# Two fixed PSUM tiles for the decays of a selective scan, each half in a bank of its own

## The chip, the core and the metric

The kernel runs on one core of one Trainium2 chip. The metric is the device time of one execution in microseconds; the figure quoted for a kernel is the median of several runs. A profile is one further execution, recorded by the hardware profiler. The engines are named as in the profile: PE (matrix products), PEld (its weight loads), DVE (vector engine), ACT (scalar engine), POOL (GpSimd), SP (the queue that issues DMAs).

## What is computed

Two layers follow each other on 32 images of 128 channels and 56 x 56 pixels, all in fp32. Layer 0 is a 7 x 7 depthwise convolution, a normalisation over channels and a routed mixture of eight small networks. Layer 1, which the change touches, holds a selective scan (Mamba) over the 3136 pixels of an image, with 256 inner channels and a state of 16 per channel:

```python
dA = jnp.exp(dt[..., None] * A)                      # decays, per channel, state and pixel
dBu = dt[..., None] * Bm[:, :, None, :] * xm[..., None]
def step(h, inp):
    dA_t, dBu_t, C_t = inp
    h = dA_t * h + dBu_t
    return (h, jnp.einsum('bds,bs->bd', h, C_t))
...
y = ys.transpose(1, 0, 2) + xm * D
return y * jax.nn.silu(z) @ out_proj_w.T
```

Around it lie a 1 x 1 convolution, a 3 x 3 depthwise branch, normalisations, Silu and softplus, and a last 1 x 1 convolution with the residual.

## The kernel before

Layer 0 runs first and leaves its result in `res_d`. `layer1` then cuts each image into 7 groups of 448 pixels (`CH1`), 224 groups in all. A group has 16 units, one for each state index (`DS`), so there are 3584 units. The 256 channels are two halves of 128 partitions; a unit's data are therefore 128 x 898: two halves of 449 elements (`W1`), the first element of each half being a carry from the group before.

One unit u passes through five steps:

- `db_pool` (line 1006, POOL) multiplies `du` and a broadcast row `bb` into `dbs[i]`, one of 16 fixed SBUF tiles, four units ahead.
- `exp_act` (line 1012, ACT) makes the decays `da`, in PSUM, with two activations, one for each half. `da` comes from the pool `pda`, which has two buffers of two banks. Half 0 fills elements 0 to 448, half 1 elements 449 to 897.
- `scan_dve` (line 1021, DVE) runs the recurrence over all 898 elements. For the ten units that are not in `POOL_C` it writes in place, into `da`. For the six units in `POOL_C` (0, 4, 6, 7, 12, 15) it writes to `hs` in SBUF.
- `cmul` (line 1027) multiplies by the broadcast row `cb` into `prod`: on DVE for in-place units, on POOL for `POOL_C` units.
- `carry_act` (line 1033, ACT) copies the last element of each half into `dbs[i]`, for the next group; in the last group of an image it copies zeros and so reads neither `da` nor `hs`. `sum_pe` (line 966, PE) adds up the products in PSUM (`py`).

The order of the work is written out by hand, step by step of a loop over t, and each engine keeps that order:

```python
if valid(t - 1):
    carry_act(t - 1)
if valid(t + 4):
    db_pool(t + 4)
if valid(t + 1):
    exp_act(t + 1)
if valid(t):
    scan_dve(t)
    if i not in POOL_C:
        cmul(t, nc.vector)
```

So in ACT's order the decays of unit t + 1 follow the carry of unit t - 1, whose buffer they can take over. The other work of a group is put into this order by `at(offset, function)`: among it `silus` (lines 837 to 854: a table load on ACT, two activations into `xm`, the product `p_z` on PE at line 843, three activations, a second table load) at unit 2 of the group before, `sp_act` (line 919, the two halves of `dt`) at unit 11, `lt_act` (line 950) at unit 13, `te_dve` (line 805, DVE) at unit 14, `yz_dve` (line 958, DVE) at unit 4. [...]

[...]

## Time and profile before

| what | value |
|---|---|
| median of 3 runs | 16874.84 us (16873.99 to 16886.92) |
| the profiled execution, its own time | 16882.28 us |
| its span, first to last instruction | 16880.3 us |
| mean granted TensorE clock | 0.905 |
| first scan begins, last scan ends | 6169.6 us, 16868.1 us |
| exponentials, line 1012 | 7168 x 639 ns |
| scans in place / into hs, line 1021 | 2240 x 2021 ns / 1344 x 2014 ns |
| products on DVE / on POOL, line 1027 | 2240 x 1092 ns / 1344 x 1932 ns |
| db on POOL, line 1006 | 3584 x 1936 ns |

In a row of the profile's groups the columns are line, engine, operation, output and inputs, shapes and count, then the busy time in us and the mean of one in ns, and last the idle time of that engine just ahead of these instructions with what ended most of it. In a timeline the columns are the start and the duration in us, engine, line, operation, and in brackets the idle time ahead of it.

### The profile page before, as it was taken

The page shows a single profiled execution, that of the slowest core. Times are in us where ns is not written, and L with a number is a line of the kernel's source. Part 1 is how long each engine was busy: PE and PEld are TensorE (multiplying, and loading weights), DVE is VectorE, ACT ScalarE, POOL GpSimd, SP SyncE. Part 2 cuts the span into 40 slices and gives each one's busy share as a digit, 9 for nine tenths or more (in the row PEclk, how much of TensorE's full clock was granted, in tenths as well). Part 3 has the DMA queues.
Part 4 walks back from the last instruction along what each step waited for, and adds up shares of the span by engine and source line. Part 5 has one row for each costly group of instructions (what it writes and reads, how often), then busy time and mean ns, then how long its engine had stood idle before and what let it go on. Part 6 is the DMA issues. An engine that isn't in the chain of part 4 may idle for free. (4 is left out here: it accounts for less than half of the span.)

```text
span 16880.3 us, 246139 instructions
## 1 busy us (share of the span) xinstructions
PE 12727.3 (75%) x91548; PEld 7010.5 (42%) x91548; DVE 11290.7 (67%) x10141; ACT 10542.4 (62%) x20754; POOL 13634.4 (81%) x9015
## 2 busy tenths in 40 slices
PE   5996200000999988888888888888888888888888
PEld 4996000000777744443444433444443444443443
DVE  1564800000111149999999999999999999999998
ACT  3564000000444458888888888888888888888887
POOL 1343067777888879999999999999999999999998
PEclk8997555555999999999999999999999999999999
DMA  9879032222555545555555555555555555555554
GB/s 255 239 231 228 7 99 84 82 85 64 70 72 71 70 101 169 171 171 168 171 172 169 171 170 170 170 171 170 172 170 170 169 171 170 172 170 170 169 171 157
DMA packets 1360754, 2533.24 MB, mean 150 GB/s; under 512 B 139119, under 2 KB 805339, under 8 KB 1355456
## 3 DMA queue, kind: packets, MB, share of 16 engines
q1 hardware_dynamic: 1163072, 2361.89, 45.3%
q0 software_dynamic: 196480, 155.61, 6.0%
q8 instruction: 720, 11.80, 0.3%
q14 instruction: 482, 3.95, 0.1%
HBM read 2180.38 MB, written 375.43 MB: 151 GB/s over the span
## 5 line engine op out<-in xcount | busy, mean ns | idle before, releaser
L1006 POOL TENSOR_TENSOR db<-du,bb 128x896 f32<-128x896 f32 x3584 | 6852.0, 1936 | 17.6
L1012 ACT ACTIVATE da<-dt,aneg 128x449 f32<-128x449 f32 x7168 | 4576.9, 639 | 603.0 <-DVE hs L1021 340.5
L1021 DVE TENSOR_TENSOR_SCAN da<-da,db 128x898 f32<-128x898 f32 x2240 | 4528.0, 2021 | 275.3 <-ACT da L1012 273.9
L1027 POOL TENSOR_TENSOR prod<-hs,cb 128x896 f32<-128x896 f32 x1344 | 2596.1, 1932 | 698.4 <-PE p_cvc L736 579.0
L966 PE MATMUL py<-prod,ident 64*64 64x448 f32 x28672 | 3099.4, 545 | 23.3 <-POOL prod L1027 16.5
L1021 DVE TENSOR_TENSOR_SCAN hs<-da,db 128x898 f32<-128x898 f32 x1344 | 2671.4, 2014 | 450.4 <-ACT db L1033 407.1
L1027 DVE TENSOR_TENSOR prod<-da,cb 128x896 f32<-128x896 f32 x2240 | 2445.7, 1092 | 216.2 <-issue 2.7
L516 ACT COPY xc<-ept 128x512 f32<-128x512 f32 (+1 forms) x248 | 144.1, 581 | 2922.6 <-DMA xb<-buf_d 2034.0
L425 POOL DMA_INDIRECT buf_d<-xg,slot x1568 | 1536.6, 980 | 485.7 <-issue 476.6
L474 POOL DMA_INDIRECT res_d<-ys,xb x984 | 1587.2, 1613 | 338.6 <-issue 286.7
L514 PE MATMUL ept<-ident,xb 128*128 128x128 f32 (+1 forms) x984 | 188.7, 274 | 2033.3 <-DMA xb<-buf_d 2033.3
L966 PEld LDWEIGHTS py<-prod,ident 64*64 64x64 f32 x28672 | 1046.2, 132 | 1444.3 <-issue 1173.5
L821 PE MATMUL p_xm<-te,wk 128*128 128x448 f32 x3584 | 1410.3, 544 | 12.3 <-DVE te L805 1.9
L422 DVE COPY xg<-gate 128x28 f32<-128x28 f32 x56 | 11.5, 233 | 1792.6 <-DMA buf_d<-xg,slot 1792.6
L466 DVE TENSOR_TENSOR ys<-py,b2t 128x512 f32<-128x512 f32 (+2 forms) x256 | 170.9, 670 | 1477.0 <-PE py L460 1269.3
L460 PEld LDWEIGHTS py<-w2t,hh 128*128 128x128 f32 x7872 | 936.2, 191 | 175.6 <-issue 113.3
L460 PE MATMUL py<-w2t,hh 128*128 128x128 f32 x7872 | 985.0, 278 | 0.3
L514 PEld LDWEIGHTS ept<-ident,xb 128*128 128x128 f32 (+1 forms) x984 | 124.6, 143 | 2037.0 <-issue 2036.9
L180 PE MATMUL pc<-xc,toep 112*112 112x112 f32 (+1 forms) x8192 | 935.8, 270 | 45.5 <-ACT toep L169 41.9
L821 PEld LDWEIGHTS p_xm<-te,wk 128*128 128x128 f32 x3584 | 657.5, 189 | 750.6 <-issue 543.1
L180 PEld LDWEIGHTS pc<-xc,toep 112*112 112x112 f32 x8192 | 881.4, 184 | 54.9 <-ACT toep L169 48.9
L210 POOL TENSOR_TENSOR xa<-xa,lng 112x896 f32<-112x896 f32 x128 | 267.3, 2088 | 773.2 <-ACT xa L207 709.7
(235 smaller groups left out, 19677.3 us busy)
## 6 DMA issues: line engine op xcount, KB each, us to landing
bb<-bc_d SPq DMA_DIRECT2D x1792, 448.0 KB
cb<-bc_d SPq DMA_DIRECT2D x1792, 448.0 KB
toep<-toep_d SPq DMA_DIRECT2D x448, 392.0 KB
xg<-res_d SPq DMA_DIRECT2D x56, 1792.0 KB
buf_d<-zero SPq DMA_DIRECT2D x14, 4550.0 KB
xb<-buf_d SPq DMA_DIRECT2D x240, 260.0 KB
xt<-in_x SPq DMA_DIRECT2D x32, 1568.0 KB
res_d<-xa SPq DMA_DIRECT2D x128, 392.0 KB
```

The source lines that it names most:

```text
L180: nc.tensor.matmul(pc[:, c, :, lo:hi], lhsT=tp[c // 2][:, c % 2, 6 - 2 * o : 8 - 2 * o, :], rhs=s4[:, c, :, lo + o - 1 : hi + o - 1], star ...
L210: nc.gpsimd.tensor_tensor(xa, xa, lng.unsqueeze(1).to_broadcast([TT, w, C]), ALU.mult)
L425: apart(nc.gpsimd.indirect_dma_start(out=buf_d[:, :], out_offset=bass.IndirectOffsetOnAxis(ap=slots[k][:, q, p0 + j : p0 + j + 1], axis=0) ...
L460: nc.tensor.matmul(py[:n, j, :], lhsT=hh[:, k, j * 128 : j * 128 + n], rhs=w2t[:, k, :], start=k == 0, stop=k == KF - 1,)
L474: apart(nc.gpsimd.indirect_dma_start(out=res_d[:, :], out_offset=bass.IndirectOffsetOnAxis(ap=xb[:n, j, C + 1 : C + 2].bitcast(I32), axis= ...
L514: nc.tensor.transpose(pt[:, j * 128 : j * 128 + n], xb[:n, j, :C], ident[:n, :n])
L821: nc.tensor.matmul(p[:, :CH1], lhsT=s["wk"][:, k, hs], rhs=d["te"][:, k : k + CH1], start=k == 0, stop=k == DC - 1 and not first,)
L966: nc.tensor.matmul(ps[r][h * HD : (h + 1) * HD, :CH1], lhsT=lhsT(rs, h), rhs=rhs[rs, h, :], start=start, stop=stop,)
L1006: nc.gpsimd.tensor_tensor(dbv[i][:, :, 1:], st[g]["du"], units[u].pop("bb"), ALU.mult)
L1012: nc.scalar.activation(da[:, h * W1 : (h + 1) * W1], st[g]["dt"][:, h, :], AF.Exp, scale=s["aneg"][:, h, i : i + 1])
L1021: nc.vector.tensor_tensor_scan(hs, da, dbs[i], 0.0, ALU.mult, ALU.add)
L1027: eng.tensor_tensor(w["prod"], w["hs"][:, :, 1:], w.pop("cb"), ALU.mult)
```

## The change

`pda` no longer rotates two buffers of one name. It holds two tiles with names of their own for the whole of layer 1, and unit u uses tile u % 2. Of each tile's 1024 elements[...] the 898 from element 63 to 960 are used[...]. The exponentials, the scan, the product and the carry work on the same shapes as before.

```diff
-        tc.tile_pool(name="pda", bufs=2, space=PSUM) as pda,
+        tc.tile_pool(name="pda", bufs=1, space=PSUM) as pda,
...
+        das = [pda.tile([128, 1024], F32, name=f"da{i}")[:, 512 - W1 : 512 + W1] for i in range(2)]
...
         def exp_act(u):
             g, i = divmod(u, DS)
-            da = units[u]["da"] = pda.tile([128, 1024], F32, name="da")
+            da = das[u % 2]
             for h in range(2):
...
         def scan_dve(u):
             i = u % DS
             w = units[u]
-            da = w.pop("da")[:, : 2 * W1]
+            da = das[u % 2]
```

## The prediction

> **What bounds the kernel now.** The change touches only layer 1's scans, so I first ask where layer 1 lies and which engine sets its pace. The page's first part gives the engines over the whole span:

> ```profile
> PE 12727.3 (75%) x91548; PEld 7010.5 (42%) x91548; DVE 11290.7 (67%) x10141; ACT 10542.4 (62%) x20754; POOL 13634.4 (81%) x9015
> ```

> Layer 1 begins with the first scan at 6169.6 us and its last scan ends at 16868.1, so 10.7 ms of the 16.88 are at stake. There DVE (VectorE) and POOL (GpSimd) both stand at nine tenths in the page's slices. The rows of the costliest groups say which of them waits for which:

> ```profile
> L1006 POOL TENSOR_TENSOR db<-du,bb 128x896 f32<-128x896 f32 x3584 | 6852.0, 1936 | 17.6
> L1012 ACT ACTIVATE da<-dt,aneg 128x449 f32<-128x449 f32 x7168 | 4576.9, 639 | 603.0 <-DVE hs L1021 340.5
> L1021 DVE TENSOR_TENSOR_SCAN da<-da,db 128x898 f32<-128x898 f32 x2240 | 4528.0, 2021 | 275.3 <-ACT da L1012 273.9
> L1027 POOL TENSOR_TENSOR prod<-hs,cb 128x896 f32<-128x896 f32 x1344 | 2596.1, 1932 | 698.4 <-PE p_cvc L736 579.0
> L1021 DVE TENSOR_TENSOR_SCAN hs<-da,db 128x898 f32<-128x898 f32 x1344 | 2671.4, 2014 | 450.4 <-ACT db L1033 407.1
> ```

> The last column is idle time ahead of the group and what ended it. POOL idles 698 us ahead of its products, and no row has DVE waiting for POOL: the decay inputs db lie ready 4 to 12 us before the scan that reads them. So DVE sets the pace and POOL follows. DVE's own idle time has two pieces: 274 us ahead of scans in place, ended by the exponentials (ACT, line 1012), and 450 us ahead of the hs scans, mostly ended by ACT too.

> Now the timeline, first DVE and then ACT, around units 12 and 13 of an ordinary group (columns: start us, us, what, idle before):

> ```profile
> 10028.05 2.02 DVE L1021 TENSOR_TENSOR_SCAN hs<-da,db 128x898 f32<-128x898 f32 x1
> 10031.50 2.04 DVE L1021 TENSOR_TENSOR_SCAN da<-da,db 128x898 f32<-128x898 f32 x1 [1.43 <-ACT da L1012]
> ```
> ```profile
> 10026.47 0.96 ACT L919 COPY dt<-p_sp 128x448 f32<-128x448 f32 x2
> ...
> 10028.17 0.16 ACT L1033 COPY db<-da 128x2 f32<-128x2 f32 x1 [0.46 <-DVE prod L1027]
> 10030.10 1.31 ACT L1012 ACTIVATE da<-dt,aneg 128x449 f32<-128x449 f32 x2 [1.77 <-DVE hs L1021]
> ```

> Unit 11's scan, product and carry are over at 10028.33, so one of the two buffers is free; yet the exponentials of unit 13 sit still for 1.77 us until unit 12's scan ends at 10030.07. That is a claim on unit 12's buffer, not on the free one: the pool has handed out the wrong one of the two, and in the built program it does so for unit 13 in 192 of 224 groups. Unit 13's scan then waits 1.43 us for decays that could have been made beside unit 12's scan. In the last group of each image, whose carries copy zeros, the same place looks different, DVE and ACT again:

> ```profile
> 11171.70 2.02 DVE L1021 TENSOR_TENSOR_SCAN hs<-da,db 128x898 f32<-128x898 f32 x1
> 11173.63 2.01 DVE L1021 TENSOR_TENSOR_SCAN da<-da,db 128x898 f32<-128x898 f32 x1
> ```
> ```profile
> 11171.82 1.31 ACT L1012 ACTIVATE da<-dt,aneg 128x449 f32<-128x449 f32 x2 [0.57 <-DVE prod L1027]
> ```

> Here the exponentials start as soon as unit 11's product ends, and the scans follow each other in 1.93 us. This is a control inside the trace: scan 12 to scan 13 takes 3.451 us in the 192 other groups and 1.934 in these 32. Whole groups (first scan to next first scan) take 47.60 and 45.76.

> The second stall comes when ACT works through the Silu block with its two table loads; the hs scan of unit 4 waits for carry 2 and its own exponentials:

> ```profile
> 10006.64 2.03 DVE L1021 TENSOR_TENSOR_SCAN hs<-da,db 128x898 f32<-128x898 f32 x1 [1.65 <-ACT db L1033]
> ```

> Scan 3 to scan 4 takes 5.86 us there, but up to 7.44 in 83 groups. The two PE timelines show why: the four p_z passes that ACT waits for take 3.07 instead of 1.77 us where the granted clock has dipped (0.58 on average over 11239 to 11243, against 1.00 over 11288 to 11292).

> ```profile
> 11239.33 3.07 PE L843 MATMUL p_z<-te,wz 128*128 128x448 f32 x4 [2.44 <-ACT xm L837]
> ```
> ```profile
> 11288.23 1.77 PE L843 MATMUL p_z<-te,wz 128*128 128x448 f32 x4 [2.44 <-ACT xm L837]
> ```

> [...]the carry (line 1033) only reads da, as the product does, and still waits for it (10028.17 above). [...]two exponentials that share no element are ordered one behind the other: the pair takes 1.31 us with 639 ns each, a gap of 33 ns, where the two dt copies of 529 ns above take 0.96, an overlap of 100. [...]the trace's slow stretches here are 3.41 us long and lie on one grid.

> **The change part by part.**

> Removed: the pool's choice. Unit 13 gets unit 11's buffer always. Its exponentials start behind carry 11 at 10028.36, end by 10029.67, and scan 12 ends at 10030.07: 0.3 us to spare before scan 13's earliest start (10029.98, since it follows an hs scan as in the control). 192 x (3.451 - 1.934) = 291 us; scan 13 itself is 2.036 now against 2.009 in the control, 192 x 0.027 = 5. **-296 us.**

> Who is late next? In the control nothing was: 13 to 14 takes 3.11, 14 to 15 takes 3.65 in both. te, lt and the carries ride on the same chain and move with it. POOL's work fills 44.7 of 47.6 us of a group (2.9 us idle at two products), so it keeps up with 45.9; its lead over the scans shrinks to what the groups behind the control already have, 4.15 us at the least.

> Removed: the wait of half 1 on half 0. An instruction that follows an exponential without a wait starts 0.06 us before its end (10026.47 against 10025.22 + 1.31), so each pair shortens by 33 + 63 = 96 ns. ACT has slack except before unit 4, where the pairs of units 3 and 4 lie on the chain: 2 x 0.096 x 224 = **-43 us**. Bounds: 0 if the wait stays, 43 if it goes.

> Moved: the data start at element 63. ACT's half 1 started at 449 before[...], at the same 639 ns as half 0, so ACT: nothing. [...]yz (line 958), the same shape[...], is 1080 ns against the product's 1092, so 0 to 12 x 2240 = 27 us of gain; I take 0.

> Added, by the new pace: clock dips. 47.60 us are 13.95 windows of 3.413, so undelayed groups drift slowly and mostly stay where PE's 2.44 us pause costs nothing; 83 groups were delayed, 88 us in all, 0.39 a group. Sorted by where scan 3 falls in its window, the delay is nothing over the first 0.42, climbs to 1.58 us at 0.84 and is gone at 0.97: a mean of 0.57 over all positions. A group of 47.60 - 1.54 - 0.19 = 45.87 us is 13.44 windows, so successive groups fall all over the window. Stepping from group to group with that curve gives 0.33 to 0.42 for the old pace (measured 0.39) and 0.58 to 0.68 for the new. I take 0.62: 224 x (0.62 - 0.39) = **+50 us**. Bounds 0.40 to 0.80: +0 to +90.

> **Sum:** -296 - 43 + 50 = -289 us against the profiled execution, 16882.28 us, which is 7.4 above the median of 16874.84. So the median becomes **16586 us**.

> **The rivals.**

> *The stall only moves* (0.03): scan 13 starts earlier but te or exponential 15 is then late by as much. Only the 43 us at unit 4 can remain, less some dips: about 16850, no change that can be measured (0.2%, 34 us, is about the least). Against it: the control.

> *The odd start costs DVE* (0.03, slower): 3584 scans and 2240 products now begin 252 bytes into a bank, and DVE is the bound. From 289 / 5824 = 50 ns each it eats the gain; at 100 ns the time is 16586 + 582 = 17168. For it: no trace row has a scan that starts there. Against: carries, products (from element 1) and ACT's half 1 already have odd starts, with no price to be seen.

> *The clock always dips* (0.05): the new pace settles at 1.58 a group: 224 x (1.58 - 0.39) = +266 in place of +50, 16802, still faster.

> *The halves' wait stays* (0.1): 16629, inside the range.

> **How the numbers follow.** The forecast with its bounds has 0.89, the halves' case included. Low end: -296 - 43 - 27 + 0 = -366, 16509. High end: -296 + 0 + 90 = -206, 16669. Faster 0.94 (forecast and dips), same 0.03, slower 0.03.

> **What would show it.** Line 1012's wait for hs gone (340 us before, mostly), line 1021 da's 275 us gone with it, pairs of exponentials at 1.21 us, POOL's idle time at 300 to 400 us, DVE's share up. Scans over 2.03 us or products over 1.10 would point to the odd start; idle time ahead of unit 13, 14 or 15 in DVE's timeline to a stall that moved; p_z passes mostly at 3 us to the clock.

## The result, and the profile after

The changed kernel takes 16631.45 us (median of 4 runs, 16628.88 to 16641.8) against 16875.24 for the kernel before: 244 us less, a ratio of 0.9855 with a 95% interval of 0.9838 to 0.9872. The profiled execution has a span of 16629.3 us. That is inside the predicted range and 45 us above the predicted 16586.

The page's rows of the costliest groups in the profile after (lines have moved by 3: 1012 is now 1015, 1021 is 1024, 1027 is 1030, 1033 is 1036):

```profile
L1015 ACT ACTIVATE da<-dt,aneg 128x449 f32<-128x449 f32 x7168 | 4577.8, 639 | 269.0 <-DVE prod L1030 86.5
L1024 DVE TENSOR_TENSOR_SCAN da<-da,db 128x898 f32<-128x898 f32 x2240 | 4523.5, 2019 | 1.6 <-ACT da L1015 1.3
L1024 DVE TENSOR_TENSOR_SCAN hs<-da,db 128x898 f32<-128x898 f32 x1344 | 2671.7, 2014 | 495.7 <-ACT db L1036 455.2
L1030 POOL TENSOR_TENSOR prod<-hs,cb 128x896 f32<-128x896 f32 x1344 | 2598.5, 1933 | 459.8 <-PE p_cvc L739 366.6
```

Read the last column against that of before. The exponentials have lost their 340 us of waiting for hs, which takes their idle time from 603 to 269 us, and the in-place scans have lost their 274 us of waiting for exponentials: 1.6 us are left of 275. POOL's idle time ahead of its products is down by 239. One row has gone the other way: the hs scans wait 496 us now, 450 before. The mean durations are within 2 ns of before.

The timelines of an ordinary group around units 12 and 13, DVE and then ACT:

```profile
10027.61 2.02 DVE L1024 TENSOR_TENSOR_SCAN hs<-da,db 128x898 f32<-128x898 f32 x1
10029.55 2.01 DVE L1024 TENSOR_TENSOR_SCAN da<-da,db 128x898 f32<-128x898 f32 x1
```
```profile
10027.73 0.16 ACT L1036 COPY db<-da 128x2 f32<-128x2 f32 x1 [0.74 <-DVE prod L1030]
10027.93 1.31 ACT L1015 ACTIVATE da<-dt,aneg 128x449 f32<-128x449 f32 x2
```

Unit 13's exponentials begin right behind carry 11 and are over at 10029.24, before scan 12 ends at 10029.63; scan 13 follows at once, 1.94 us after scan 12, as in the last groups of the images before. But the pair of exponentials still takes 1.31 us: half 1 still starts 33 ns behind the end of half 0.

Where the 245 us of layer 1 (first to last scan, 10696.5 to 10451.4 us) lie, from the starts of the scans in the two traces, summed over the 224 groups, in us:

| step | before | after | difference |
|---|---|---|---|
| scan 12 to scan 13 | 724.4 | 434.5 | -289.9 |
| scan 13 to scan 14 | 701.3 | 696.9 | -4.4 |
| scan 3 to scan 4 | 1391.8 | 1436.5 | +44.7 |
| the 13 others together | 7879.0 | 7883.4 | +4.4 |

Undelayed steps from scan 3 to scan 4 would add up to 1303.8 us over the 224 groups. What a trace has above that is called the excess below: 88.0 us before, 132.8 after.

### The profile page after: what moved, and what is told of

It reads as the page before. It is cut to its first block, busy times and chain, and to the rows that moved or that the text cites. A ratio compares the mean times of both kernels' runs of the same rounds, so it can differ in the third digit from the quotient of the medians.

```text
span 16629.3 us, 245915 instructions
## 1 busy us (share of the span) xinstructions
PE 12779.3 (77%) x91548; PEld 7009.9 (42%) x91548; DVE 11272.7 (68%) x10141; ACT 10556.5 (63%) x20754; POOL 13631.4 (82%) x9015
## 5 line engine op out<-in xcount | busy, mean ns | idle before, releaser
L1009 POOL TENSOR_TENSOR db<-du,bb 128x896 f32<-128x896 f32 x3584 | 6854.7, 1937 | 17.6
L1024 DVE TENSOR_TENSOR_SCAN da<-da,db 128x898 f32<-128x898 f32 x2240 | 4523.5, 2019 | 1.6 <-ACT da L1015 1.3
L1024 DVE TENSOR_TENSOR_SCAN hs<-da,db 128x898 f32<-128x898 f32 x1344 | 2671.7, 2014 | 495.7 <-ACT db L1036 455.2
L1030 DVE TENSOR_TENSOR prod<-da,cb 128x896 f32<-128x896 f32 x2240 | 2446.1, 1092 | 219.4 <-issue 5.3
```

Of the source, the lines that this page charges most:

```text
L1009: nc.gpsimd.tensor_tensor(dbv[i][:, :, 1:], st[g]["du"], units[u].pop("bb"), ALU.mult)
L1024: nc.vector.tensor_tensor_scan(hs, da, dbs[i], 0.0, ALU.mult, ALU.add)
L1030: eng.tensor_tensor(w["prod"], w["hs"][:, :, 1:], w.pop("cb"), ALU.mult)
```

## The experiments

Three versions of the story were to be told apart: that only the choice of the buffer counts (the theory), that the place of the halves in the tile counts too (half 1 begins with element 449 in the kernel before, with 512 in the changed one), and that a fixed tile has cheaper waits than one taken from a pool. Then the two terms of the sum that stay unclear: the clock dips and the wait inside a pair. A trace has the granted clock in records, 258 in the trace of before and 336 in that of after. Each is at 1.0 or at 0.5, and each but the last, which ends with the trace, lasts a whole multiple of 3.413 us, so that all of a trace lie on one grid. A dip is a stretch at 0.5; in layer 1 there are 86 before, 82 of them of 3.41 us, and 130 after, 126 of them of 3.41 us. The groups of runs came from several chips, whose medians for the kernel before lie between 16867 and 16907 us; so times are set against the kernel before of the same group, and across groups I compare the length of layer 1 in the traces.

**Fixed tiles, data from element 0**

```diff
-        das = [pda.tile([128, 1024], F32, name=f"da{i}")[:, 512 - W1 : 512 + W1] for i in range(2)]
+        das = [pda.tile([128, 1024], F32, name=f"da{i}")[:, : 2 * W1] for i in range(2)]
```

> Two fixed tiles in turn, but the data from element 0 as before[...]. Theory (the choice of the buffer is the whole gain, the place of the data is worth nothing): as the changed kernel, 16631 us within 30, scan 12 to scan 13 in 1.93 us, exponentials 33 ns apart. Rival (the place of the halves carries part of the gain): slower than 16631 by its share, at most back to 16875.

16630.34 us, against 16867.32 for the kernel before (ratio 0.9859, 0.9843 to 0.9876). Scan 12 to 13 takes 1.934 us, and the exponentials of a pair lie 33 ns apart, as in the kernel before and in the changed one. The place of the halves is worth nothing that can be measured: 0.9859 here, 0.9855 for the change.

**The pool as before, data from element 63**

```diff
-            da = units[u]["da"] = pda.tile([128, 1024], F32, name="da")
+            da = units[u]["da"] = pda.tile([128, 1024], F32, name="da")[:, 512 - W1 : 512 + W1]
...
-            da = w.pop("da")[:, : 2 * W1]
+            da = w.pop("da")
```

> The rotating pool of two buffers as before, but the data from element 63[...]. Theory: unit 13 gets unit 12's buffer again, scan 12 to scan 13 in 3.45 us, 16875 us within 30. Rival (the place of the halves matters): part of the 244 us is there without fixed tiles, below 16840.

16872.59 us (12 runs, one of them 17037), ratio 1.0009 (0.9992 to 1.0027). The rows of its page show both old waits, 603.1 and 275.2 us for 603.0 and 275.3:

```profile
L1012 ACT ACTIVATE da<-dt,aneg 128x449 f32<-128x449 f32 x7168 | 4576.7, 638 | 603.1 <-DVE hs L1021 340.5
L1021 DVE TENSOR_TENSOR_SCAN da<-da,db 128x898 f32<-128x898 f32 x2240 | 4528.5, 2022 | 275.2 <-ACT da L1012 275.2
```

With the place of the data changed and the pool kept, nothing is gained (1.0009); with the pool changed and the place kept, everything (0.9859).

**A fresh tile for each unit, but two names**

```diff
-        tc.tile_pool(name="pda", bufs=2, space=PSUM) as pda,
+        tc.tile_pool(name="pda", bufs=1, space=PSUM) as pda,
...
-            da = units[u]["da"] = pda.tile([128, 1024], F32, name="da")
+            da = units[u]["da"] = pda.tile([128, 1024], F32, name=f"da{u % 2}")
```

> No fixed tiles: each unit takes a fresh tile from the pool, but even and odd units have names of their own with one buffer each, data from element 0. Only the choice of the buffer differs from the kernel before. Theory: as the changed kernel, 16631 us within 30. Rival (a tile that lives throughout has cheaper waits than one that is taken and given back): stays nearer to 16875.

16627.04 us, ratio 0.9858 (0.9842 to 0.9875): the whole gain without a fixed tile. Its in-place scans idle for 1.6 us in all:

```profile
L1021 DVE TENSOR_TENSOR_SCAN da<-da,db 128x898 f32<-128x898 f32 x2240 | 4523.6, 2019 | 1.6 <-ACT da L1012 1.5
```

So what paid is that unit 13 can't be given unit 12's buffer; taking and giving back costs nothing here (16627.04 us against 16630.34 for the fixed tiles from element 0).

**PE kept busy in the pause ahead of p_z**

```diff
+                if g > 1:
+                    for k in range(5):
+                        nc.tensor.matmul(
+                            st[g - 2]["py"][:, k % 2, CH1:512], lhsT=ident, rhs=ident[:, : 512 - CH1], start=True, stop=True
+                        )
                 ps = []
                 for h in range(2):
                     p = mm_tile("p_z")
```

> The changed kernel, with five extra small products on PE in the pause ahead of p_z (into columns of py that nobody reads), so that PE is not idle for 2.4 us there. Theory (long steps from scan 3 to scan 4 come from the clock dips that this pause brings on, 148 us in all after the change, 88 before): the dips at p_z go, that step is 5.86 us in nearly all groups, 16631 - 148 = 16483 us, within 30. Rival (the clock is not the cause, or so short a filling does not count): 16631 us or a little more.

16496.69 us, ratio 0.9779 (0.9763 to 0.9796), 134 us less than the kernel of the same group with fixed tiles from element 0 and no products. The expectation named 148 us of dips; by the excess defined above it is 133. PE's timeline in this kernel, the five extra products (two records each) and p_z behind them:

```profile
9954.10 1.33 PE L845 MATMUL py<-ident 128*128 128x64 f32 x10
9956.40 1.77 PE L851 MATMUL p_z<-te,wz 128*128 128x448 f32 x4 [0.96 <-ACT xm L840]
```

and its row of the hs scans:

```profile
L1029 DVE TENSOR_TENSOR_SCAN hs<-da,db 128x898 f32<-128x898 f32 x1344 | 2669.9, 2014 | 360.8 <-ACT db L1041 323.5
```

The pause falls from 2.23 to 0.96 us, p_z takes the 1.77 us that it takes where the clock is at 1.0, and the hs scans wait 361 us in place of 496. Steps from scan 3 to scan 4 that are over 0.1 us too long: 5 of 224, against 126 in the changed kernel; the excess over all 224 is 0.6 us, against 133. Of the kernels that leave nothing out this is the fastest.

**The same products in the kernel before**

The edit is the one above, made in the kernel before.

> The kernel before, with the same five small products on PE in the pause ahead of p_z. Theory (the kernel before lost 88 us to dips there, and without dips the choice of the buffer is worth 192 x 1.517 + 192 x 0.027 = 296 us): 16875 - 88 = 16787 us, that is 290 to 300 above the 16497 of the changed kernel with these products. Rival (dips are as costly before as after, 148): near 16730, and the gain without dips only some 240.

16835.3 us against 16906.81 (ratio 0.9957, 0.9941 to 0.9974): 72 us less, where 88 was forecast; the 16787 us of the expectation are missed, in part because the kernel before is itself 32 us slower in this group. Layer 1 takes 10618.3 us; of the 88.0 us of excess in the kernel before, 12.5 are left, with 15 long steps. Against 10315.1 us for the changed kernel with the products the difference is 303, of which 12 are those leftovers: 291 for the choice of the buffer alone. The rival, equal dips before and after and a gain of some 240, is out.

**Half 1 shortened by what the wait costs**

```diff
+                n = W1 - 115 if h == 1 and i in (3, 4) else W1
                 nc.scalar.activation(
-                    da[:, h * W1 : (h + 1) * W1], st[g]["dt"][:, h, :], AF.Exp, scale=s["aneg"][:, h, i : i + 1]
+                    da[:, h * W1 : h * W1 + n], st[g]["dt"][:, h, :n], AF.Exp, scale=s["aneg"][:, h, i : i + 1]
                 )
```

> The changed kernel; for units 3 and 4 the exponential of half 1 makes only the first 334 of its 449 elements (115 left out, the rest of the half keeps old values), which shortens each of these two pairs by about the 96 ns that the wait of half 1 on half 0 was priced at. Theory (that wait is still in the changed kernel, and its price on the chain ahead of unit 4 is the 43 us that the forecast counted): scan 3 to scan 4 in 5.67 us where no dip falls, 16631 - 43 = 16588 us, up to 20 either way from the dips. Rival (something else is late next ahead of unit 4): 5.86 us stays, 16631.

16599.46 us, 307 below the kernel before of its group (ratio 0.9814, 0.9798 to 0.983), where the change alone is 244 below. Layer 1 takes 10397.2 us, 54 less than after the change, where 43 was forecast; undelayed steps from scan 3 to scan 4 are 5.67 us. The dips blur this by some 10 us, so the next run is the cleaner one.

> The same short exponentials of half 1 of units 3 and 4 (115 of 449 elements left out), together with the five small products on PE in the pause, so that clock dips don't blur the result. Theory: 16497 - 43 = 16454 us within 10, step 3 to 4 in 5.67 us. Rival: 16497.

16486.12 us, ratio 0.975 (0.9734 to 0.9766). The expected 16454 is missed as an absolute time, in a group whose kernel before is 39 us slower than in the group with the products alone; so the lengths of layer 1 decide: 10270.2 us, 44.9 less than with the products alone, where 43 was forecast. The DVE timeline at unit 4, in the changed kernel and in this one:

```profile
10005.85 2.03 DVE L1024 TENSOR_TENSOR_SCAN hs<-da,db 128x898 f32<-128x898 f32 x1 [1.64 <-ACT db L1036]
```

```profile
9974.48 1.08 DVE L966 TENSOR_TENSOR yz<-py,zs 128x896 f32<-128x896 f32 x1
9977.01 2.03 DVE L1030 TENSOR_TENSOR_SCAN hs<-da,db 128x898 f32<-128x898 f32 x1 [1.45 <-ACT db L1042]
```

The stall ahead of unit 4 is 1.45 us where it was 1.64: two times 0.1 us on ACT comes out on DVE in full. So the forecast was right in what two pairs shorter by 96 ns are worth. That a pair without the wait would be shorter by 96 ns is not shown, as the wait was not taken away.

**One and two products in the pause**

The edit is again the one above, with `range(1)` and `range(2)`; one run each, with a profile.

> The changed kernel with one extra small product on PE in the pause ahead of p_z (0.27 us of work), so that about 1.97 us of 2.23 are left idle. If any shortening helps in proportion, the dips cost about 133 x (1 - 0.27 / 1.33) = 106 us; if a pause must stay under some length, still about 133, so 16600 to 16631 us.

> The same with two extra products, about 1.70 us idle. In proportion: 80 us of dips are left, near 16577 us. With a limit between 1.2 us (never delayed in the last groups of the images) and 2.2: either nothing is left, 16498, or all of it, 16631.

| extra products | pause ahead of p_z, us | long steps, of 224 | excess over all 224, us |
|---|---|---|---|
| 0 | 2.23 | 126 | 132.8 |
| 1 | 1.86 | 117 | 118.2 |
| 2 | 1.64 | 74 | 78.1 |
| 5 | 0.96 | 5 | 0.6 |

16640.42 and 16598.45 us, next to 16896.56 for the kernel before. One product shows no effect beyond the scatter: its 118.2 us lie among the 117.4, 121.8 and 132.8 of the three kernels without products and with the same pause (element 0, two names, the change itself). Two products leave 78.1 us, close to the 80 in proportion, so a limit on the length of the pause that leaves all or nothing does not fit; each of the two is a single run.

## Why the prediction was right, and where it was off

**What bounds layer 1.** Right. DVE sets the pace: 245 us taken out of its chain are 244 us of the kernel, and POOL, whose idle time fell from 698 to 460 us, never became the bound. The sign named for it, 300 to 400 us, was not reached; in the kernel with the products it is 320.

**The pool's choice, -296 us.** Measured -289.9 for the step and -4.4 for the shorter scan 13: -294. The control inside the trace of before (the last group of each image) had given the new step to the nanosecond, 1.934 us. Nothing else was late in its place; "the stall only moves" is out. The two-name kernel shows that it was the choice of the buffer and not the fixed tile.

**The wait of half 1 on half 0, -43 us.** This step failed: measured 0. I had taken for granted that the wait comes from the place of half 1 in the tile, and so goes when half 1 begins with element 512. The after timeline has 1.31 us for a pair as before, not the 1.21 named as the sign. In the trace of the changed kernel half 1 carries a wait on the semaphore that half 0 raises in all 3584 pairs, and starts 33 ns behind its end, both as in the trace of before. So the two writes of ACT into one tile are ordered one behind the other in both places; why they are was not shown, and neither was that the place has a part in it. No trace or run here shows where a bank ends: what they compare is data from element 0 and from element 63. The case that the wait stays was in the range, at 0.1; it should have been the larger one, as no row of before showed a pair without the wait. A kernel with the wait itself taken away was not tried; the shortened halves only show what two pairs shorter by 0.1 us bring, 45 us.

**The dips, +50 us.** Measured +44.7; 132.8 us in 224 groups are 0.59 a group, for the forecast 0.62. That it came so close is in part luck: the kernels with element 0 and with two names have the same pause and pace, and there the term is +29 and +34. The reasoning holds in its parts: sorted by where scan 3 falls in the window of 3.413 us, 133 of 219 groups before lie in the free part of the window (the first 0.42), 68 after; in the part up to 0.84 a group loses 0.82 us before and 0.87 after. The products on PE show that PE's idleness in the pause is the cause: 132.8 us of excess without them, 0.6 with five. One thing I had overlooked: the last group of an image is never delayed. Behind its pause of 1.21 us no stretch of half clock follows: in the windows of 3.41 us that the pause touches, PE's records still fill a share of at least 0.64, above the 0.41 of the experiments. The PE timelines of an ordinary and of a last group after the change:

```profile
10000.49 1.77 PE L846 MATMUL p_z<-te,wz 128*128 128x448 f32 x4 [2.23 <-ACT xm L840]
```
```profile
10046.70 1.77 PE L846 MATMUL p_z<-te,wz 128*128 128x448 f32 x4 [1.21 <-ACT xm L840]
```

**The odd start and the unbroken rows, 0.** Right: scans 2019 and 2014 ns, products 1092 ns, the same with data from element 0 and from element 63. The products are no shorter with their data from element 63, so the 12 ns by which yz is shorter have nothing to do with the place.

**The sum.** -294 + 0 + 45 + 4 for the other steps = -245, where the forecast had -296 - 43 + 50 = -289. The miss of 44 is in effect the one term: the others are off by 2, 5 and 4 us and cancel to 1. The rival "the halves' wait stays" had named 16629, 2 us from what was measured; with dips that differ by 15 us between like kernels, so close a hit is luck too.

## What to carry to other kernels

Two buffers of one name are not two buffers in turn: the pool may hand out the one that was used last, here to unit 13 in 192 of 224 groups (3.451 us from scan 12 to scan 13, 1.934 in the other 32), and the new work then waits for the newest reader in place of the oldest. By what rule the pool chose was not looked into. It shows as a wait on a step that should lie one unit further back; here names of their own (16627.04 us) or fixed tiles (16630.34 us) settled it, where the pool of one name took 16867.32 in the same group. And before a wait is counted as removed, look in the trace of before for the same two operations without it: there was none.

## What was not expected of the hardware

In the changed kernel PE pauses ahead of p_z once in 46 us, for 2.23 us in an ordinary group, and is busy for 9399 of the 10451 us of layer 1. Still p_z ran, at least in part, at a granted clock of 0.5 in 125 of 224 groups; behind a pause of 1.21 us it did so in none of 31. Since the half-clock stretches of a trace lie on one grid of 3.413 us, a faster loop can meet them more often than a slower one: when the undelayed group went from 47.60 us (13.95 windows) to 46.06 (13.49), the excess rose from 88 us to between 117 and 133. Five small products that compute nothing gave back 134 us, over half of what the change itself did.
